# A graph-network layer on one core: two node streams laid in halves of the partitions, or in even and odd partitions

## The chip, the cores and the metric

The kernel runs on one core of a Trainium2 chip. The metric is the device time of one execution in microseconds; the time before is the median of three executions, 485.97 us (483.73 to 487.27).

## The reference

There are 12500 nodes with 128 features (`x`) and 412500 edges with 48 features (`edge_attr_48`), and each edge has a receiving node `dst`. The edges come sorted by `dst`.

```
agg = segment_sum(edge_attr_48, dst, 12500)          # 12500 x 48
h   = relu(layernorm(x))                             # 12500 x 128
u   = graph_globals[0]                               # one vector of 64 for all nodes
hid = relu(concat([h, agg, u]) @ W1 + b1)            # 12500 x 256
out = x + hid @ W2 + b2                              # 12500 x 128
```

Everything is float32.

## The kernel before

**Edges.** The edges are cut into 403 chunks of 1024, and these into two streams: stream 0 takes the first half of the chunks, stream 1 the second. A step (`contract`, L370) takes one chunk of each stream. A chunk's segment sum is a matmul of the edge features against a 0/1 matrix (`oh`, written by VectorE at L365 from the relative receiver numbers `rel`), gathered in PSUM (`ps`, L377); a step has 32 matmul instructions on TensorE. Six steps make a group; after a group VectorE adds `ps` into `aggT` (L393), which holds stream 0's sums in partitions 0 to 47 and stream 1's in partitions 64 to 111. There are 34 groups, so 204 steps. Edge features come in tiles `e` of two chunks, 384 KB each, through SyncE's DMA queue (L151); 15 tiles are in flight or in use at a time, and the next load is issued when TensorE has used a tile up.

**Nodes.** As the sums come in, the nodes are worked off in blocks. A block has 512 nodes (256 in the first and the last): half of them from the beginning of stream 0's nodes and half from stream 1's, which lie `END` rows farther in memory. There are 25 such blocks and one of 212 nodes from the middle. A node block is a tile of 128 partitions in which each partition holds four nodes in a row (2048 bytes); in the kernel before, partitions 0 to 63 hold stream 0's nodes and partitions 64 to 127 stream 1's. So one DMA of `x` (L221, on ScalarE's queue) or of results `ot` (L597, on SyncE's queue, the same that loads the edges) has two runs of 64 rows in device memory; the function `both` (L204) writes this access pattern with the two streams as its outermost dimension.

For a block, VectorE takes statistics (L517), ScalarE normalizes (`xn`, L513), TensorE transposes (`pt`, L529), ScalarE copies the transposed block from PSUM to `hT` (L533) with the nodes in order of partition and place in the partition, so that stream 0's nodes are the first half of the columns. TensorE makes the hidden layer in PSUM (`ph`): `hidden_x` (L553) from `hT`, `hidden_sums` (L566) from `aggT`, one half of the columns from each stream. ScalarE applies the bias and relu and writes `hid` (L573) with the columns sorted by place and then by partition. `output` (L585) uses `hid` as weights, 64 columns at a time, and `store` (L590) adds `x + b2` and issues the DMA of the results. `ot` has two buffers.

**Order.** The order on each engine is written out by hand: the loop at L717 goes through the steps; after each step a credit allows some of the node pieces (`pieces`, L613 on). The first three loads of `x` are issued on ScalarE's queue ahead of the first copies of `rel` (L438), which the first 0/1 matrices need.

Of the kernel before, what the change touches and what calls it, by code (L numbers as in the profile page):

```python
# [16 lines left out]
P = 128  # L17
# [4 lines left out]
def kernel(  # L22
# [31 lines left out]
    nc = tc.nc  # L54
    N, D = x.shape
# [33 lines left out]
    PH = P // 2  # L89
# [8 lines left out]
    NB2 = len(sizes)  # L98
    MID = sum(sizes) * PH
    NM = N - 2 * MID  # L100
    END = MID + NM
# [101 lines left out]

    def both(ap, a, r):  # L204

        return bass.AP(tensor=ap.tensor, offset=ap.offset + a * D, ap=[[END * D, 2], [r * D, PH], [1, r * D]])

    xs, xts, xns, xbs, hTs, hids, pos = {}, {}, {}, {}, {}, {}, {}
    x_loads = []

    def load_x(k):

        if k >= len(pairs):
            return
        xt = xp.tile([P, 2, R * D], F32, name="xt")
        xts[k] = xt

        def load(i, j):
            a, m, r = blocks[j]
            if j < NB2:  # L220
                nc.scalar.dma_start(xt[:, i, :r * D], both(x, a, r))  # L221
                return
            f = m - m % 16
            nc.scalar.dma_start(xt[:f, i, :r * D], rows_of(x, a, f, r))
            if f < m:
                nc.scalar.dma_start(xt[f:m, i, :r * D], rows_of(x, a + f * r, m - f, r))

        for i, j in enumerate(pairs[k]):
            xs[j] = xt[:, i].rearrange("p (r d) -> p r d", d=D)
            x_loads.append((k, lambda i=i, j=j: load(i, j), max(step, min(16 * k - 32, 114 + 4 * k))))  # L230
# [51 lines left out]
    with nc.allow_non_contiguous_dma(reason="a few hundred numbers, once"):  # L282
        for s in range(2):
            mid0 = C0[s] * CE
            n = min(NI, (E - mid0) // GE)
# [3 lines left out]
            for i in range(n, NI):  # L289
                m = mid0 + i * GE + GE // 2  # L290
# [233 lines left out]
    def transpose(j):  # L524
        _, m, nr = blocks[j]
        pt = pst.tile([P, R, P], F32, name="pt")
        xn = xns.pop(j)
        for r in range(nr):
            nc.tensor.transpose(pt[:, r, :m], xn[:m, r], ident[:m, :m])  # L529

        hT = mp.tile([P, BN], F32, name="hT", bufs=4)
        hTs[j] = hT[:, :m * nr]
        nc.scalar.copy(hTs[j].rearrange("d (p r) -> d p r", r=nr), pt[:, :nr, :m].rearrange("d r p -> d p r"))  # L533

    phs = {}

# [19 lines left out]
    def hidden_sums(j, q):  # L556

        at, m, nr = blocks[j]
        n = nr * PH
        if j < NB2:  # L560
            for s in range(2):
                a = s ^ q
                h = slice(s * HI, s * HI + DE)
                f = s * END + at + shift[s]
                for c in (0, HI):
                    nc.tensor.matmul(phs[j, a][c:c + HI, s * n:(s + 1) * n], w1a[h, a * P + c:a * P + c + HI],  # L566
                                     aggT[h, f:f + n], start=False, stop=True, skip_group_check=True)
        else:
            for c in (0, HI):
                nc.tensor.matmul(phs[j, q][c:c + HI, :NM], w1a[:K2, q * P + c:q * P + c + HI], mid[:K2],  # L570
                                 start=False, stop=True, skip_group_check=True)
        for a, h, f in ((q, 0, PH), (1 - q, PH, P)) if j < NB2 else ((q, 0, m),):
            nc.scalar.activation(hids[j][:, a, :nr, h:f],  # L573
                                 phs[j, a][:, h * nr:f * nr].rearrange("h (p r) -> h r p", r=nr),
                                 AF.Relu, bias=bias[:, a:a + 1])

    def output(j, r):
# [12 lines left out]
    def store(j):  # L590
        a0, m, nr = blocks[j]
        ot = mp.tile([P, R, D], F32, name="ot")
        nc.vector.tensor_tensor(ot[:m, :nr], pos.pop(j)[:m, :nr], xbs.pop(j)[:m, :nr], OP.add)  # L593
        k = m - m % 16
        od = ot[:, :nr].rearrange("p r d -> p (r d)")
        if j < NB2:
            nc.sync.dma_start(both(out, a0, nr), od)  # L597
            return
        nc.sync.dma_start(rows_of(out, a0, k, nr), od[:k])
        if k < m:  # L600
            nc.scalar.dma_start(rows_of(out, a0 + k * nr, m - k, nr), od[k:m])
# [20 lines left out]
    for j in range(NB2 + 1):  # L622
        if j == NB2:
            pieces.append((at[j], 0.0, lambda: copy_middle(0)))
        pieces.append((at[j], 0.6 * size[j], lambda j=j: hidden_sums(j, 0)))
        for q in [j + 2] if j + 3 < NB2 else [NB2 - 1, NB2] if j + 3 == NB2 else []:
            pieces.append((at[j], 0.8 * size[q], lambda q=q: turn(q)))
        pieces.append((at[j], 0.6 * size[j], lambda j=j: hidden_sums(j, 1)))
        if j < NB2:
            piece_x(j + 1, 0)  # L630
        for r in range(blocks[j][2]):
            pieces.append((at[j], 0.45, lambda j=j, r=r: output(j, r)))
        if j < NB2:
            piece_x(j + 1, 1)
# [22 lines left out]
    def turn(j):  # L657
        nonlocal turned
        while not normalized(j):
            next_part(True)  # L660
        transpose(j)
        turned = j
# [54 lines left out]
    for step in range(CG * NI + 3):  # L717
        i, k = divmod(step, CG)
# [30 lines left out]
    with tc.If(isbad >= 1):  # L749
# [63 lines left out]
        for k, js in enumerate(pairs):  # L813
            load_x(k)
            while x_loads:
                next_x()
            normalization(k)
            while parts:
                parts.pop(0)[2]()
            for j in js:  # L820
                transpose(j)
            for j in js:
                for a in range(NH):
                    hidden_x(j, a)
                for q in range(2):
                    hidden_sums(j, q)
                for r in range(blocks[j][2]):
                    output(j, r)
                store_late()
# [28 lines left out]
```

## Time and profile before

| what | before |
|---|---|
| median of three executions | 485.97 us |
| the profiled execution's own time | 485.91 us |
| its span | 484.1 us |
| granted TensorE clock, mean | 0.868 |
| TensorE matmul, VectorE, ScalarE busy | 341.8, 242.6, 123.6 us |
| DMA bytes, mean rate | 95.39 MB, 197 GB/s |

The span is the time between the first and the last instruction; the execution's own time is 1.8 us longer. The busy time of an engine is the union of its instructions. The DMA share is the mean over the core's 16 DMA engines: a share of 0.13 is what two engines of sixteen give when they are always busy (2/16 = 0.125).

### The profile page before, as it was taken

The page shows a single profiled execution, that of the slowest core. Times are in us where ns is not written, and L with a number is a line of the kernel's source. Part 1 is how long each engine was busy: PE and PEld are TensorE (multiplying, and loading weights), DVE is VectorE, ACT ScalarE, POOL GpSimd, SP SyncE. Part 2 cuts the span into 40 slices and gives each one's busy share as a digit, 9 for nine tenths or more (in the row PEclk, how much of TensorE's full clock was granted, in tenths as well). Part 3 has the DMA queues.
Part 4 walks back from the last instruction along what each step waited for, and adds up shares of the span by engine and source line. Part 5 has one row for each costly group of instructions (what it writes and reads, how often), then busy time and mean ns, then how long its engine had stood idle before and what let it go on. Part 6 is the DMA issues. An engine that isn't in the chain of part 4 may idle for free.

```text
span 484.1 us, 17713 instructions
## 1 busy us (share of the span) xinstructions
PE 341.8 (71%) x8037; PEld 272.4 (56%) x8038; DVE 242.6 (50%) x415; ACT 123.6 (26%) x296; POOL 15.5 (3%) x54
## 2 busy tenths in 40 slices
PE   6476839839796609949578706964956996599982
PEld 5475718727575408748456605744834864387751
DVE  1687516914763605825555524751734663767230
ACT  2143121423122105042023003321214131252220
POOL 9200000000000000000000000000000000000000
PEclk9986978978989958979969776995985999799997
DMA  8729594993566565765655765594665767786111
GB/s 240 252 80 268 175 290 123 318 301 122 184 207 199 198 183 190 244 229 172 210 177 175 234 201 196 179 313 140 197 206 171 237 204 221 218 253 237 56 40 43
DMA packets 62441, 95.39 MB, mean 197 GB/s; under 512 B 3755, under 2 KB 55831, under 8 KB 62356
## 3 DMA queue, kind: packets, MB, share of 16 engines
q1 hardware_dynamic: 58590, 87.16, 57.4%
q10 hardware_dynamic: 3382, 6.51, 3.6%
q8 instruction: 65, 1.06, 0.9%
q0 software_dynamic: 384, 0.49, 0.4%
q14 instruction: 20, 0.16, 0.1%
HBM read 87.74 MB, written 6.40 MB: 194 GB/s over the span
## 4 chain that ended last, share of the span: by engine, by line
DMA 56%; PE 32%; ACT 4%; DVE 3%; issue 1%; ACTq 1%; SPq 1%; POOL 0%; DVEq 0%; POOLq 0%
DMA e<-in_edge_attr_dram 45%; PE ps L377 17%; DMA xt<-in_x_dram 6%; PE po L585 6%; PE ph L553 5%; DMA out_dram<-ot 4%; PE ph L566 3%; DVE oh L365 2%; ACT xn L513 2%; ACT hid L573 1%; PE pt L529 1%; ACTq L221 1%; SPq L151 1%; DVE ot L593 0%; PE po L336 0%
## 5 line engine op out<-in xcount | busy, mean ns | idle before, releaser
L377 PEld LDWEIGHTS ps<-oh,e 128*48 128x48 f32 x6448 | 189.1, 133 | 85.7 <-issue 49.7
L377 PE MATMUL ps<-oh,e 128*48 128x44 f32 (+1 forms) x6448 | 198.8, 224 | 31.6 <-DMA e<-in_edge_attr_dram 20.0
L365 DVE TENSOR_TENSOR oh<-iota,rel 128x2816 f32<-128x2816 f32 (+3 forms) x72 | 149.8, 2100 | 26.6 <-ACT rel L439 25.6
L585 PE MATMUL po<-w,hid 128*64 128x128 f32 (+1 forms) x784 | 66.6, 295 | 26.2 <-ACT hid L573 26.0
L393 DVE TENSOR_TENSOR aggT<-aggT,ps 48x201 f32 (+1 forms) x68 | 24.4, 359 | 111.3 <-PE ps L377 79.9
L513 ACT ACTIVATE xn<-xt,sh,sc 128x128 f32<-128x128 f32 (+1 forms) x100 | 42.9, 485 | 112.9 <-DMA e<-in_edge_attr_dram 96.1
L585 PEld LDWEIGHTS po<-w,hid 128*64 128x64 f32 (+1 forms) x784 | 49.9, 148 | 29.0 <-ACT hid L573 27.9
L573 ACT ACTIVATE hid<-ph,bias 128x256 f32<-128x256 f32 (+2 forms) x102 | 41.5, 458 | 80.8 <-PE ph L566 65.9
L566 PE MATMUL ph<-aggT,w1a 48*64 48x256 f32 (+1 forms) x400 | 36.0, 421 | 34.3 <-ACT hid L573 28.4
L553 PE MATMUL ph<-hT,w1h 128*64 128x512 f32 (+2 forms) x208 | 58.5, 633 | 0.0
L593 DVE TENSOR_TENSOR ot<-po,xb 128x512 f32<-128x512 f32 (+2 forms) x26 | 17.4, 671 | 40.1 <-PE po L585 35.1
L529 PE MATMUL pt<-ident,xn 128*128 128x128 f32 (+1 forms) x100 | 19.6, 303 | 22.9 <-ACT xn L513 13.7
L517 DVE BATCH_NORM_STATS2 st<-xt 128x6 f32<-128x128 f32 (+1 forms) x100 | 23.6, 281 | 22.5 <-DMA xt<-in_x_dram 22.5
L566 PEld LDWEIGHTS ph<-aggT,w1a 48*64 48x64 f32 x400 | 11.6, 139 | 40.2 <-ACT hid L573 33.9
L503 ACT ACTIVATE sc<-va,eps 128x8 f32<-128x8 f32 (+3 forms) x15 | 4.5, 299 | 94.8 <-DVE va L502 94.8
L529 PEld LDWEIGHTS pt<-ident,xn 128*128 128x128 f32 (+1 forms) x100 | 11.3, 145 | 27.0 <-ACT xn L513 16.6
L533 ACT COPY hT<-pt 128x512 f32<-128x512 f32 (+2 forms) x26 | 14.4, 553 | 14.6 <-PE pt L529 8.1
L547 DVE TENSOR_TENSOR xb<-xt,b_sb 128x1024 f32<-128x1024 f32 (+3 forms) x15 | 15.6, 1038 | 0.1
L553 PEld LDWEIGHTS ph<-hT,w1h 128*64 128x64 f32 x208 | 13.5, 151 | 0.8 <-issue 0.6
L445 PE MATMUL pt<-ident,df 108*128 108x108 f32 (+3 forms) x36 | 6.6, 312 | 9.8 <-ACT hT L533 9.7
L445 PEld LDWEIGHTS pt<-ident,df 108*128 108x128 f32 (+3 forms) x36 | 4.9, 203 | 10.6 <-ACT hT L533 9.8
L438 ACT COPY rel<-pt 128x216 f32<-128x216 f32 (+3 forms) x9 | 4.0, 444 | 20.2 <-issue 10.9
(89 smaller groups left out, 89.8 us busy)
## 6 DMA issues: line engine op xcount, KB each, us to landing
e<-in_edge_attr_dram SPq DMA_DIRECT2D x200, 384.0 KB
xt<-in_x_dram ACTq DMA_DIRECT2D x23, 256.0 KB
out_dram<-ot SPq DMA_DIRECT2D x23, 256.0 KB
di<-in_dst_dram SPq DMA_DIRECT2D x4, 216.0 KB
e<-in_edge_attr_dram SPq DMA_DIRECT2D x2, 192.0 KB
di<-in_dst_dram SPq DMA_DIRECT2D x2, 180.0 KB
di<-in_dst_dram SPq DMA_DIRECT2D x2, 144.0 KB
xt<-in_x_dram ACTq DMA_DIRECT2D x2, 128.0 KB
```

The lines of the kernel that those rows point to most:

```text
L365: nc.vector.tensor_tensor(hots[i][:, at:at + n * Q * w].rearrange("p (h q w) -> p h q w", h=n, w=w)[:, :, q], iota[:, None, None, :w].to_b ...
L377: nc.tensor.matmul(ps[s * HI:s * HI + DE, o:o + WID[k]], edges[c][0][:, t * DE:(t + 1) * DE], hot(i, s, k, t), start=(k == 0 and t == 0), ...
L393: nc.vector.tensor_tensor(to, to, acc[i % len(acc)][h, :wg], OP.add)
L513: nc.scalar.activation(xns[j][:m, r], xs[j][:m, r], AF.Relu, bias=sh[:m, c:c + 1], scale=sc[:m, c:c + 1])
L517: parts.append((k, None, lambda i=i, j=j, r=r: nc.vector.bn_stats(st[:m, i * nr + r, :], xs[j][:m, r, :])))
L529: nc.tensor.transpose(pt[:, r, :m], xn[:m, r], ident[:m, :m])
L547: nc.vector.tensor_tensor(xb[:m, :n, :nr], xts[k].rearrange("p i (r d) -> p i r d", d=D)[:m, :n, :nr], b2_sb[:m, None, None, :].to_broadca ...
L553: nc.tensor.matmul(phs[j, a][c:c + HI, :nr * m], w1h[:, a * P + c:a * P + c + HI], hTs[j], start=True, stop=False, skip_group_check=True)
L566: nc.tensor.matmul(phs[j, a][c:c + HI, s * n:(s + 1) * n], w1a[h, a * P + c:a * P + c + HI], aggT[h, f:f + n], start=False, stop=True, ski ...
L573: nc.scalar.activation(hids[j][:, a, :nr, h:f], phs[j, a][:, h * nr:f * nr].rearrange("h (p r) -> h r p", r=nr), AF.Relu, bias=bias[:, a:a ...
L585: nc.tensor.matmul(pos[j][c:k, r], hids[j][:, a, r, c:k], w2[:, a], start=(a == 0), stop=(a == NH - 1), skip_group_check=True)
L593: nc.vector.tensor_tensor(ot[:m, :nr], pos.pop(j)[:m, :nr], xbs.pop(j)[:m, :nr], OP.add)
```

## The change

The streams' nodes of a block change places within the tile. Partition 2i now holds what partition i held (stream 0), and partition 2i + 1 what partition 64 + i held (stream 1). Three places follow: the pattern of the DMAs of `x` and of results has the 64 rows as its outermost dimension and the two streams inside it; the copy to `hT` puts the even partitions' nodes in the first half of the columns and the odd ones' in the second, so that the matmuls of the hidden layer stay as they were; and the activation that writes `hid` writes each half of the columns to every second column instead of to 64 neighbours. Each engine has as many instructions as before, in the same order, and each DMA as many bytes in rows of the same length.

```diff
     def both(ap, a, r):
 
-        return bass.AP(tensor=ap.tensor, offset=ap.offset + a * D, ap=[[END * D, 2], [r * D, PH], [1, r * D]])
+        return bass.AP(tensor=ap.tensor, offset=ap.offset + a * D, ap=[[r * D, PH], [END * D, 2], [1, r * D]])
...
         hTs[j] = hT[:, :m * nr]
-        nc.scalar.copy(hTs[j].rearrange("d (p r) -> d p r", r=nr), pt[:, :nr, :m].rearrange("d r p -> d p r"))
+        n = 2 if j < NB2 else 1
+        nc.scalar.copy(hTs[j].rearrange("d (s p r) -> d s p r", s=n, r=nr),
+                       pt[:, :nr, :m].rearrange("d r (p s) -> d s p r", s=n))
...
-        for a, h, f in ((q, 0, PH), (1 - q, PH, P)) if j < NB2 else ((q, 0, m),):
-            nc.scalar.activation(hids[j][:, a, :nr, h:f],
-                                 phs[j, a][:, h * nr:f * nr].rearrange("h (p r) -> h r p", r=nr),
+        for a, s in ((q, 0), (1 - q, 1)) if j < NB2 else ((q, 0),):
+            k = 2 if j < NB2 else 1
+            f = m // k * nr
+            nc.scalar.activation(hids[j][:, a, :nr, s:m:k],
+                                 phs[j, a][:, s * f:(s + 1) * f].rearrange("h (p r) -> h r p", r=nr),
                                  AF.Relu, bias=bias[:, a:a + 1])
```

## The prediction

> **What bounds the kernel now.** I read the page's time slices first, then the table of windows, then the chain of waits, then ScalarE's timeline at the start.
>
> ```profile
> PE   6476839839796609949578706964956996599982
> ...
> DMA  8729594993566565765655765594665767786111
> ...
> q1 hardware_dynamic: 58590, 87.16, 57.4%
> q10 hardware_dynamic: 3382, 6.51, 3.6%
> q8 instruction: 65, 1.06, 0.9%
> ...
> DMA 56%; PE 32%; ACT 4%; DVE 3%; issue 1%; ACTq 1%; SPq 1%; POOL 0%; DVEq 0%; POOLq 0%
> ```
>
> The chain that ended last is 56% DMA, yet the DMA engines are only 57.4 + 3.6 + 0.9 + 0.4 + 0.1 = 62.4% busy, and TensorE falls to 3 or 4 tenths again and again. A bound of DMA with more than a third of it idle means either latency or uneven load. The table of windows tells which (columns: stretch, length, busy time and instructions of PE, PEld, DVE, ACT, POOL, then granted clock, DMA share, GB/s):
>
> ```profile
> 328.00:332.00 4.00, 0.00 (x0) 0.00 (x0) 0.00 (x0) 0.00 (x0) 0.00 (x0) 0.59 0.13 49
> 452.00:460.00 8.00, 8.00 (x179) 5.50 (x175) 2.96 (x12) 2.28 (x6) 0.00 (x0) 1.00 0.15 56
> 54.00:66.00 12.00, 7.83 (x222) 6.41 (x222) 8.06 (x16) 0.30 (x1) 0.00 (x0) 0.99 0.97 318
> 312.00:322.00 10.00, 7.92 (x212) 6.10 (x210) 8.25 (x15) 3.12 (x8) 0.00 (x0) 1.00 1.02 349
> ```
>
> From 328 to 332 every compute engine stands still, waiting for edges, while DMA moves 49 GB/s at a share of 0.13: two engines of sixteen. From 452 to 460 the edges are in, only results are being stored, and again it is about two (0.15, instruction fetches included). Where edges flow alone (54 to 66) the share is 0.97 at 318 GB/s: an edge load uses all sixteen. So a DMA of `x` or of results runs on two engines, and an edge tile has a sixteenth of its bytes on each of those two; it has not landed before they have come to it.
>
> Are these two engines full? Page part 6 lists 23 loads of `x` of 256 KB and 2 of 128 KB, and the same number of stores: 12.6 MB, at 49 GB/s 257 us. The edges, 202 tiles of 384 KB, are 79 MB; two sixteenths are 9.9 MB, at 49 GB/s 202 us. Together 459 of 484.1 us. These two engines are the bound of the whole kernel; nearly every long wait for edges is a wait for them. (That the edges are spread evenly is inferred from the share of 0.97.)
>
> The Trainium skill, "DMA: Bandwidth & Descriptors", section "Why a DMA increments its semaphore by 16 and not by 1", gives the count for both versions, where the trace can show only the first: the largest number up to 16 that divides the outermost dimension on both sides, so 2 before (2 and 128) and 16 after (64 and 128). No run here shows the second yet; by the rule the forecast below holds, and without it the third rival stays open.
>
> **The change, part by part.**
>
> *The DMAs.* The trace has two rows for how wide a transfer is: a pattern with 2 as its outermost dimension runs on two engines, the edge loads' pattern, with 128 partitions outermost, on all sixteen. The new pattern has 64, which can be dealt out to sixteen; I take sixteen for the fifty transfers, with two as the other end (rival 3). The number, bytes, row length and issuing queue stay. A transfer of 256 KB, 5.3 us at 49 GB/s, then takes 0.75 to 0.82 us at 349 to 318 GB/s plus its latency. The load per engine becomes the mean, 62.4% of 484.1 = 302 us. Bounds by rate: 95.39 MB at 349 and 318 GB/s give 273 and 300 us.
>
> *The start.* ScalarE's timeline:
>
> ```profile
> 5.42 11.10 ACTq L221 DMA_DIRECT2D xt<-in_x_dram  x3
> 16.56 0.24 ACT L438 COPY rel<-pt 128x48 f32<-128x48 f32 x1 [10.90 <-issue]
> ```
>
> Issuing three loads holds ScalarE for 11.1 us, since the two engines' queues are full; an unhindered issue takes 0.51 us (the median of L221), so 1.5 us. `rel` comes 9.6 us earlier, and with it the 0/1 matrices and the first `ps` matmul, which stood at 18.23 us: about 9 us. What is late next is the edges: at the 268 GB/s of the first 20 us some 2.4 MB, six tiles, are there by then, enough.
>
> *The copy to `hT`* (26 of 553 ns) reads two interleaved halves; its reading was already strided, so I take it at nothing. *The activation to `hid`* (102 of 458 ns) writes every second column. The trace has no such write. Dense: the copy to `hT` of 212 columns at 0.34 us; far apart: `rel`, 216 columns at 516 ns. The difference, 0.8 ns a column, bounds it: 0 to 0.2 us each, 0 to 21 us on ScalarE, which is busy 124 us and hides it. Without cover, at the end of the kernel where some eight stand on the path, it is 0 to 1.7 us. I take 0, the stride of two being nearest to dense.
>
> *A wait that is added.* The first `output` matmuls of a block read 64 neighbouring columns of `hid`, written before by one activation, now by two. Queued behind them on TensorE are the following `ps` matmuls. Between the last activation and them stands `hidden_x` (0.88 us in the chain), longer than two activations (0.84 us): nothing in midstream, about 0.1 us for each of three blocks at the end. On SyncE's, ScalarE's and GpSimd's queues nothing changes place.
>
> **The sum.** With the two engines relieved, TensorE is next. Its pace without waits stands in the chain (start, length, what):
>
> ```profile
> 298.31 0.71 PE ps L377 x32
> 299.02 0.89 PE po L585 x16
> ...
> 304.56 0.59 PE ph L566 x8
> 305.15 0.85 PE ps L377 x32
> 306.00 0.59 PE pt L529 x4
> ...
> 308.89 0.88 PE ph L553 x4
> 309.76 0.71 PE ps L377 x32
> ```
>
> From 298.31 to 309.76 it makes eight steps with all node work of one block: 11.45/8 = 1.43 us a step, at full clock. 202 steps' worth of matmuls (6448/32): 289 us. The transposes of `dst` come on top (L445, 6.6 us) and the first dozen steps have no node work; I let these cancel. But in that stretch DMA was half idle. Coupling costs something: TensorE was busy 19.57 of 20 us with DMA share 0.33 (440 to 460), but 18.53 and 18.19 with 0.82 and 0.77:
>
> ```profile
> 80.00:100.00 20.00, 18.53 (x524) 15.20 (x518) 15.26 (x26) 5.91 (x12) 0.00 (x0) 1.00 0.82 266
> 420.00:440.00 20.00, 18.19 (x524) 15.80 (x520) 13.60 (x24) 8.45 (x19) 0.42 (x1) 0.98 0.77 242
> 440.00:460.00 20.00, 19.57 (x491) 14.69 (x488) 8.68 (x25) 6.37 (x16) 0.00 (x0) 1.00 0.33 119
> ```
>
> That is 6.6%, 19 us. The end, from the last `ps` (458.8) to 484.1, is 25.3 us; in the chain a store on two engines holds an `ot` buffer there for 7.80 us, while the matmuls of the last block end at 474.9 instead of 476.4, so only 1.5 us go: 24. Sum: 9 + 289 + 19 + 24 = 341 us of span, plus 1.8 us around it: **343 us**, against 485.91 us for the profiled execution (the median, 485.97, is the same). DMA by itself: 2 + 302 to the last bytes, of which the last blocks' stores lie behind, then the end: about 329. VectorE, 242.6 us busy, is 71% of the new span and not the bound.
>
> On the clock: it fell to 0.66 from 280 to 300 and 0.74 from 320 to 340, where TensorE had long waits, and was 1.00 from 440 to 460, where it worked nearly without a break. The Trainium skill, "TensorE: Matmul & The Clock Gate", section "Part 1: The HAM clock gate", agrees (half clock after an idle window of about 3.4 us) and speaks against a full clock here: waits of that length that remain would keep the gate closing. By it the sum is 343 us if they go, near the first rival's time if they stay.
>
> **Rivals.**
>
> 1. *The clock stays as it is.* For: waits for edges may go on in shorter pieces; mean 0.868 before. Against: the waits come from two engines that are no longer overloaded. 289/0.868 = 333; 9 + 333 + 19 + 24 + 2 = 387 us.
> 2. *DMA remains the bound, by its busiest engine.* Instruction fetches (q8: 0.9% of sixteen engines, 70 us) come one at a time; if one engine carries them all, it has 302 - 4 + 70 = 368 us, and with the end 2 + 368 + 24 + 2 = 396 us. For: one engine is enough to hold a tile back. Against: nothing shows that one engine carries them.
> 3. *It doesn't do what it says*: the queue still cuts the transfer into two runs of engines. Then 459 us on the same two engines and 486 us. Against: the 128-partition edge loads are spread.
> 4. *Slower.* TensorE, now busy nearly all the time, is held at a low clock by its own load. 289/c + 54 passes 486 where c falls below 0.67; at half clock through 632 us. Place: the step loop from 20 us on. Against: clock 0.98 and 1.00 in the two rows from 420 to 460, with TensorE busy 37.8 of 40 us. From 0.67 downward it decides.
>
> **How the numbers follow.** Chances: forecast 0.78; the clock 0.09; the busiest engine 0.09; no effect 0.02; low clock 0.02. The range takes in the forecast without coupling (324), a start and DMA slightly better (318), and reaches past the first two rivals: 318 to 400. A measurement of this kernel tells about 1% from no change. Faster by over 1%: 0.78 + 0.09 + 0.09 = 0.96; within: 0.02; slower: 0.02.
>
> **What would show it.** Right: the DMA share no longer stays at 0.13 with compute engines idle; three loads of `x` issued within 2 us and the first `ps` matmul near 9 us; the chain mostly TensorE; mean clock above 0.93; rate near 280 GB/s; `hid` near 458 ns. Wrong: stretches of DMA share 0.13 remaining (rival 3); a share near 0.06 with TensorE waiting (one engine, rival 2); clock below 0.9 with TensorE busy (1 or 4); `hid` at 0.6 us or more (the write's price).

## The result and the profile after

The changed kernel takes 354.14 us (350.9 to 356.11, four executions) against 485.45 us before (483.73 to 487.27): a ratio of 0.7288, 95% interval 0.7227 to 0.7349. In a second measurement it was 0.7240 (0.7204 to 0.7276). Forecast were 343 us, in a range of 318 to 400. The profiled execution took 354.23 us, its span 352.4 us; 131.7 us of span are gone. Executions of one kernel differ by up to 3%: a ratio is taken from the fast ones alone (within 1.5% of the fastest), a time in us is the median of all.

The lines of the page that answer to those shown of before (TensorE and DMA in 40 slices, the DMA queues, the chain that ended last):

```profile
PE   7794979999999899899998889989999999999881
...
DMA  7999997999999998998799899999989898921010
...
q1 hardware_dynamic: 58940, 87.16, 75.9%
q10 hardware_dynamic: 3732, 6.51, 5.6%
q8 instruction: 65, 1.06, 1.3%
...
PE 74%; DVE 11%; issue 6%; ACT 4%; DMA 2%; SPq 1%; DVEq 0%; ACTq 0%
```

The bytes are the same. TensorE falls to 4 tenths once, in the fourth slice (26 to 35 us), and stays at 7 or more after that until the last slice; DMA is at 7 to 9 tenths until the edges are in; and the chain has turned round: DMA from 56% to 2%, TensorE from 32% to 74%. The DMA engines' mean load, 83.4% of 352.4 us (75.9 + 5.6 + 1.3 + 0.5 + 0.1), is 294 us; before it was 302. So there is no less DMA work; it is spread.

The windows (stretch, length, busy time and instructions of PE, PEld, DVE, ACT, POOL, granted clock, DMA share, GB/s):

```profile
20.00:40.00 20.00, 14.98 (x382) 12.27 (x378) 17.46 (x51) 9.38 (x24) 0.00 (x0) 0.91 1.06 374
240.00:260.00 20.00, 19.93 (x532) 16.17 (x529) 14.91 (x24) 7.42 (x20) 0.00 (x0) 1.00 0.91 292
320.00:340.00 20.00, 17.93 (x353) 12.43 (x347) 6.47 (x18) 4.81 (x13) 0.00 (x0) 1.00 0.10 34
```

From 240 to 260 us TensorE is busy 19.93 of 20 us at full clock with DMA at a share of 0.91; that is the best of these rows, the worst from 60 to 300 us has 17.57 busy. The only long stretch with little DMA is the end, where the edges are in; no DMA stands on the chain there any more.

ScalarE at the start, and TensorE's first and last `ps` matmuls in the timeline (start, length):

```profile
6.74 2.98 ACTq L221 DMA_DIRECT2D xt<-in_x_dram  x3
9.76 0.24 ACT L438 COPY rel<-pt 128x48 f32<-128x48 f32 x1 [4.09 <-DMA e<-in_edge_attr_dram]
...
11.44 4.06 PE L377 MATMUL ps<-oh,e 128*48 128x44 f32 x96 [3.14 <-DVE oh L365]
...
327.93 0.91 PE L377 MATMUL ps<-oh,e 128*48 128x37 f32 x16
```

Three loads of `x` are issued in 2.98 us instead of 11.10. The first `ps` matmul is at 11.44 us (18.23 before), the last ends at 328.8 (458.8), and 23.6 us follow.

ScalarE's groups by shape (count, busy us, mean ns), then the issue of `x` (minimum, median, maximum in ns):

```profile
L577 ACT ACTIVATE hid<-ph,bias 128x256 f32<-128x256 f32 x92 | 39.9, 489 | 68.6 <-PE ph L568 68.6
L534 ACT COPY hT<-pt 128x512 f32<-128x512 f32 x23 | 13.3, 580 | 8.5 <-PE pt L529 8.5
...
L221 ACTq DMA_DIRECT2D xt<-in_x_dram x25: 542/542/750, 6.7 to 277.3; - x25
```

The strided write of `hid` costs 22 ns an instruction (467 before), the copy to `hT` 2 ns (578 before), and no issue of `x` takes longer than 0.75 us, where before the longest took 7.6.

### The profile page after: what moved, and what is told of

Its sections match the earlier page's. It is cut to its first block, busy times and chain, and to the rows that moved or that the text cites. A ratio compares the mean times of both kernels' runs of the same rounds, so it can differ in the third digit from the quotient of the medians.

```text
span 352.4 us, 17715 instructions
## 1 busy us (share of the span) xinstructions
PE 317.1 (90%) x8037; PEld 254.5 (72%) x8038; DVE 242.0 (69%) x415; ACT 124.8 (35%) x296; POOL 15.5 (4%) x54
## 3 DMA queue, kind: packets, MB, share of 16 engines
q1 hardware_dynamic: 58940, 87.16, 75.9%
## 4 chain that ended last, share of the span: by engine, by line
PE 74%; DVE 11%; issue 6%; ACT 4%; DMA 2%; SPq 1%; DVEq 0%; ACTq 0%
PE ps L377 37%; PE po L589 13%; PE ph L555 11%; PE ph L568 8%; DVE oh L365 6%; PE pt L529 4%; ACT hid L577 2%; DMA e<-in_edge_attr_dram 2%; DVE st L517 1%; ACT xn L513 1%; DVE aggT L393 1%; PE pt L445 1%; DVE ot L597 1%; ACT sc L503 0%; DVE va L502 0%
## 5 line engine op out<-in xcount | busy, mean ns | idle before, releaser
L377 PEld LDWEIGHTS ps<-oh,e 128*48 128x48 f32 x6448 | 177.9, 127 | 64.0 <-issue 55.0
L377 PE MATMUL ps<-oh,e 128*48 128x44 f32 (+1 forms) x6448 | 188.9, 218 | 14.7 <-issue 10.9
L577 ACT ACTIVATE hid<-ph,bias 128x256 f32<-128x256 f32 (+2 forms) x102 | 43.3, 479 | 75.5 <-PE ph L568 73.7
L589 PE MATMUL po<-w,hid 128*64 128x128 f32 (+1 forms) x784 | 58.5, 278 | 1.2 <-ACT hid L577 1.1
L555 PE MATMUL ph<-hT,w1h 128*64 128x512 f32 (+2 forms) x208 | 53.7, 591 | 0.0
L589 PEld LDWEIGHTS po<-w,hid 128*64 128x64 f32 (+1 forms) x784 | 43.4, 137 | 3.7 <-ACT hid L577 2.6
L568 PE MATMUL ph<-aggT,w1a 48*64 48x256 f32 (+1 forms) x400 | 34.1, 398 | 2.9 <-ACT hid L577 2.8
L529 PE MATMUL pt<-ident,xn 128*128 128x128 f32 (+1 forms) x100 | 17.9, 296 | 7.0 <-ACT xn L513 6.9
L534 ACT COPY hT<-pt 128x512 f32<-128x512 f32 (+2 forms) x26 | 14.4, 554 | 9.5 <-PE pt L529 9.5
L568 PEld LDWEIGHTS ph<-aggT,w1a 48*64 48x64 f32 x400 | 10.9, 132 | 8.5 <-ACT hid L577 3.6
L555 PEld LDWEIGHTS ph<-hT,w1h 128*64 128x64 f32 x208 | 11.8, 142 | 1.1 <-issue 0.9
L336 PE MATMUL po<-ident 128*128 128x128 f32 x24 | 5.2, 387 | 2.0 <-POOL ident masks.py:199 2.0
```

Of the source, the lines that this page charges most:

```text
L377: nc.tensor.matmul(ps[s * HI:s * HI + DE, o:o + WID[k]], edges[c][0][:, t * DE:(t + 1) * DE], hot(i, s, k, t), start=(k == 0 and t == 0), ...
L555: nc.tensor.matmul(phs[j, a][c:c + HI, :nr * m], w1h[:, a * P + c:a * P + c + HI], hTs[j], start=True, stop=False, skip_group_check=True)
L577: nc.scalar.activation(hids[j][:, a, :nr, s:m:k], phs[j, a][:, s * f:(s + 1) * f].rearrange("h (p r) -> h r p", r=nr), AF.Relu, bias=bias[ ...
L589: nc.tensor.matmul(pos[j][c:k, r], hids[j][:, a, r, c:k], w2[:, a], start=(a == 0), stop=(a == NH - 1), skip_group_check=True)
```

## The experiments

All ratios are to the kernel before, measured beside it. "In halves" means that each DMA is issued as two, one for each half of the partitions.

| kernel | us | ratio (95%) |
|---|---|---|
| changed kernel, second measurement | 354.77 | 0.7240 (0.7204 to 0.7276) |
| both transfers in two halves | 371.56 | 0.7624 (0.7576 to 0.7673) |
| only results in halves (x on two engines) | 425.74 | 0.8775 (0.8740 to 0.8810) |
| only x in halves (results on two engines) | 388.03 | 0.7991 (0.7961 to 0.8020) |
| halves, but every fourth block on two engines | 387.89 | 0.7971 (0.7927 to 0.8015) |
| x twice | 371.83 | 0.7606 (0.7567 to 0.7645) |
| x twice but in the first blocks | 366.73 | 0.7539 (0.7517 to 0.7561) |
| half of the last matmul | 342.56 | 0.7032 (0.6989 to 0.7076) |
| first x issued later | 354.51 | 0.7307 (0.7277 to 0.7337) |
| two combs (two DMAs, each to every second partition) | 364.17 | 0.7450 (0.7419 to 0.7482) |
| two halves, first x issued later | 370.62 | 0.7626 (0.7606 to 0.7645) |
| only results in halves, x ahead | 436.52 | 0.9009 (0.8987 to 0.9031) |

### Is it the number of engines, or the new order of the rows?

In the layout of before, each transfer is issued as two, so that 64 becomes the outermost dimension without any change of places.

```diff
-                nc.scalar.dma_start(xt[:, i, :r * D], both(x, a, r))
+                for s in range(2):
+                    nc.scalar.dma_start(xt[s * PH:(s + 1) * PH, i, :r * D], stream(x, a, r, s))
...
-            nc.sync.dma_start(both(out, a0, nr), od)
+            for s in range(2):
+                nc.sync.dma_start(stream(out, a0, nr, s), od[s * PH:(s + 1) * PH])
```

`stream(ap, a, r, s)` is the 64 rows of one stream.

> The layout of before is kept (streams in the halves of the partitions, hid written densely), but each DMA of x and of results is issued as two, one for each stream, of 64 rows. Theory (number of engines): each half goes over sixteen engines, so the load per engine is that of the changed kernel: 350 to 362 us; the 50 further issues of about 0.54 us on ScalarE's and SyncE's queues are hidden. Rival (it is the pairing of near and far rows, or the dense reading of neighbouring partitions, that helps): close to the time before, 470 to 487 us.

371.56 us. The rival is out: with the old layout and a dense `hid`, 114 of the 131 us are gained by the pattern of the DMAs alone, although their number doubles. But the time lies 10 us above the theory's range; the next sections follow that up.

### One of the two alone

The same edit for the results only, and for `x` only.

> The layout of before; only the DMAs of results are issued as two of 64 rows, x stays as before. Theory (load of two engines): 9.9 MB of edges and 6.3 MB of x at 49 GB/s are 330 us on the two engines, plus the end of 24 us, with some coupling: 355 to 395 us. Rival (what costs is that ScalarE is held while it issues x): nearly the time before, 450 us or more.

> The layout of before; only the DMAs of x are issued as two of 64 rows, results stay as before. Theory (load of two engines): the same 330 us on the two engines, so about the same time as with only the results divided, 355 to 395 us, the start 7 us earlier and the end some 2 us longer. Rival (ScalarE held by issuing x): nearly all of the gain, 350 to 360 us.

425.74 and 388.03 us. With only `x` divided the time is in the range; with only the results divided it is 31 us above it. Neither rival fits: ScalarE's holding would have given about 355 us with `x` divided. Against the run with both divided, results on two engines cost 16 us, `x` on two engines 54 us, both together 114 us (485.88 - 371.56), more than the sum of 71. That fits two engines that are full only with both (an estimated 459 us of load with both, 330 with one). That equal bytes cost so unequally, the load alone doesn't explain. What held SyncE's issues of edges (line, releaser, us in total, times, longest) in the run with `x` on two engines, and then in the one with results on two:

```profile
SPq L151 <- DMA xt<-in_x_dram: 98.3, 19, 8.6
```

```profile
SPq L151 <- DMA out_dram<-ot: 38.5, 14, 3.6
```

The same work waits 98.3 us for `x` in the one and 38.5 for results in the other. The two runs also differ in when these transfers are made. Step 50 begins at 119.3 us with `x` on two engines, at 99.2 with results on two and at 98.8 with both divided: 20 of the 54 us are lost by then, after ten loads of `x` issued 1 to 33 us apart, and nothing in the other run, where the first of four stores comes at 52 us. Whether this bunching makes the difference was not tried.

### Is x late?

In the run with `x` on two engines VectorE's statistics waited 18.2 us for `x`. So there the loads of `x` were made due ten steps earlier, and the normalization was to stay at its old step.

```diff
-            ... max(step, min(16 * k - 32, 114 + 4 * k))))
+            ... max(step, min(16 * k - 42, 104 + 4 * k))))
...
-                begun in came and ... and came[begun] <= step - 8)):
+                begun in came and ... and came[begun] <= step - 18)):
```

> The run with only the results divided (x on two engines, 425.7 us), with each load of x due ten steps earlier and the normalization at the same step as there. Theory (x on two engines costs more than results on two because its transfer, some 14.5 us in the chain, is longer than its lead, and normalization and TensorE wait for it): 390 to 410 us. Rival (x costs more because it is on another queue and halves the two engines' pace for the edges): 420 to 430 us.

436.52 us: slower, and outside both ranges. The waits of VectorE's statistics for `x` are gone from the list of waits, and SyncE's issues wait as they did, now 109.6 us for `x`:

```profile
SPq L151 <- DMA xt<-in_x_dram: 109.6, 16, 8.7
...
SPq L602 <- DMA xt<-in_x_dram: 20.8, 5, 6.7
```

The loss lies at the start. The first five loads of `x` are issued at the same steps in both runs, so for them the edit only held the normalization back. ScalarE's normalization in the run with `x` on two engines, and then in this one (instructions, duration, first and last start):

```profile
L517 ACT ACTIVATE xn<-xt,sh,sc x100: 477/484/500, 30.0 to 388.2; 128x128 f32<-128x128 f32 x96, 53x128 f32<-53x128 f32 x4
```

```profile
L517 ACT ACTIVATE xn<-xt,sh,sc x100: 477/485/497, 40.4 to 399.0; 128x128 f32<-128x128 f32 x96, 53x128 f32<-53x128 f32 x4
```

It begins 10.4 us later and ends 10.8 us later. Step 20 begins at 68.0 us instead of 56.6, and from there to the end both runs take the same time, 365.9 and 366.7 us, although most loads in between are issued 7 to 16 steps earlier. So it is not lateness of `x`: earlier loads gain nothing. The rival, competition between the two queues on the two engines, fits that, but wasn't tried by itself (by giving `x` the edges' queue). Why `x` costs more than three times what results cost on two engines is left open.

### Does a transfer on two engines cost in proportion, or only above a limit?

Both transfers in halves, except in every fourth block (6 of 25).

```diff
+                if j % 4 == 1:
+                    nc.scalar.dma_start(xt[:, i, :r * D], both(x, a, r))
+                    return
```

and the same for the results.

> The layout of before; x and results are issued as two of 64 rows except in every fourth block (6 of 25), where they stay on two engines. Theory (load of two engines, no cost below the pace of TensorE): 9.9 + 3.1 MB at 49 GB/s are 266 us, below TensorE's 320 us, so 350 to 364 us. Rival (each transfer on two engines costs its own delay, in proportion): 354 plus a quarter of the 131 us, about 385 us.

387.89 us. Against its proper base, the run with two halves (371.56), 16 us for 24% of the transfers, where proportion would be 27 us of 114. The theory that nothing is lost while the two engines' total load stays below TensorE's time is refuted: with a load of 266 us in 384 there were still waits (the chain by line):

```profile
PE ps L385 34%; PE po L593 12%; PE ph L561 10%; DMA xt<-in_x_dram 10%; PE ph L574 7%; DMA e<-in_edge_attr_dram 7%; PE pt L537 3%; DVE oh L373 1%; ACT hid L581 1%; ACT xn L521 1%; PE pt L453 1%; DVE st L525 1%; ACTq L229 0%; DVE ot L601 0%; ACT hT L541 0%
```

In the run with two halves, with no transfer on two engines, the same line reads:

```profile
PE ps L382 32%; PE po L590 11%; PE ph L558 10%; DMA e<-in_edge_attr_dram 8%; PE ph L571 7%; DVE oh L370 3%; PE pt L534 3%; ACT xn L518 2%; ACT hid L578 2%; DMA xt<-in_x_dram 2%; DVE st L522 1%; DMA di<-in_dst_dram 1%; DVE ot L598 1%; PE pt L450 1%; ACTq L226 1%
```

So the edges' share has not risen; that of `x` has, from 2% to 10%. Its pieces on the chain (start, length) all lie in the first 65 us; the first and the third are the first two loads left on two engines:

```profile
8.60 18.32 DMA xt<-in_x_dram
32.11 5.84 DMA xt<-in_x_dram
50.62 13.92 DMA xt<-in_x_dram
```

Step 30 begins at 78.6 us here and at 69.0 in the run with two halves (spans 383.9 and 372.0), so most of the loss between these two profiles is there early; what each later transfer cost can't be told from them. A mean load is a lower bound here, no forecast.

### What bounds the changed kernel: TensorE or DMA?

DMA work was added: each load of `x` a second time, into a tile that nobody reads. And TensorE work was taken away: half of the last matmul.

```diff
                 nc.scalar.dma_start(xt[:, i, :r * D], both(x, a, r))
+                again = xp.tile([P, R * D], F32, name="again", bufs=2)
+                nc.scalar.dma_start(again[:, :r * D], both(x, a, r))
```

```diff
-        for a in range(NH):
+        for a in range(1):
...
-                nc.tensor.matmul(pos[j][c:k, r], hids[j][:, a, r, c:k], w2[:, a], start=(a == 0), stop=(a == NH - 1),
+                nc.tensor.matmul(pos[j][c:k, r], hids[j][:, a, r, c:k], w2[:, a], start=(a == 0), stop=True,
```

> The changed kernel with each DMA of x issued a second time into a tile that nobody reads: 6.3 MB more. Theory (TensorE sets the pace, DMA has room): 0 to 5 us more than the changed kernel. Rival (DMA still sets the pace): 6.6% more bytes, 15 to 20 us more.

> The changed kernel without the second half of the hidden columns in the last matmul: 392 of its 784 matmul instructions are left out, so the results lack that half. They cost 1.81 us per 32 in the chain, so 22 us. Theory (TensorE sets the pace): 15 to 22 us less than the changed kernel. Rival (DMA or VectorE sets the pace): 0 to 5 us less.

> The changed kernel once more, as the measure for the other runs of this call: 351 to 356 us.

371.83, 342.56 and 354.77 us. The added transfers cost 5.1% (0.7606/0.7240; 4.4% against the first measurement's 0.7288), as the rival said; the removed matmuls gave 10 (by the ratios) to 12 of 22 us, between both ranges. But doubling also put three more issues ahead of `rel`, so it was repeated without the first three blocks:

> The changed kernel with the DMAs of x issued a second time into a tile that nobody reads, but not in the first three blocks, so that nothing more stands ahead of rel: 5.6 MB more. Theory (most of the 17 us that the doubling cost came from the issues ahead of rel, and TensorE sets the pace afterwards): 353 to 361 us. Rival (the bytes cost it, DMA sets the pace as well): 366 to 372 us.

366.73 us, 4.1% more (0.7539/0.7240; 3.4% against 0.7288) for 5.9% more bytes: most of the cost is not the start's. Bytes and issues are not parted by this. The 22 added issues hold ScalarE for 16.1 us, and the run with two combs below, with 50 issues more and no more bytes, is 8 to 10 us above the changed kernel. The stretch from 60 to 300 us of the changed kernel, of x twice, and of half of the last matmul:

```profile
60.00:300.00 240.00, 227.99 (x6115) 183.45 (x6113) 178.96 (x287) 90.32 (x212) 0.18 (x1) 1.00 0.92 300
```

```profile
60.00:300.00 240.00, 222.09 (x5883) 178.09 (x5880) 173.94 (x271) 85.86 (x203) 0.18 (x1) 0.99 0.95 312
```

```profile
60.00:300.00 240.00, 219.75 (x5902) 172.81 (x5896) 184.82 (x288) 93.77 (x219) 0.18 (x1) 0.97 0.93 307
```

With more DMA work TensorE is busy 6 us less in these 240, and with less of its own 8 us less; DMA rises to 0.95 and 0.93. Part of the 6 us is spread: in the second measurement's profile of the changed kernel itself TensorE is busy 224.51 us, with DMA at 0.91. The changed kernel stands near two limits, TensorE at 95% and DMA at 92%, and neither alone sets the pace: work on DMA's side costs time, and work taken from TensorE gives back only half of its own. What TensorE waits for in midstream the profile doesn't show (10.9 us before `ps`, with no releaser).

### The start

In the changed kernel the three issues of `x` still stand ahead of `rel`. They were put behind it, in the changed kernel and in the one with two halves.

```diff
-    for _ in range(3):
-        next_x()
     stir(5)
     spread(0, dfs[0], start=True)
+    for _ in range(3):
+        next_x()
```

> The changed kernel with the first three loads of x issued on ScalarE's queue after the first copies of rel instead of before. In the changed kernel these issues hold rel until 9.76 us although the transposes are done at about 7.4. Theory (the start is on the path): first ps matmul 2 to 3 us earlier, 1 to 3 us less time. Rival (the start is hidden by the edges' arrival, or x comes late for the first block): no difference, or 1 to 2 us more.

> The run with two halves again, with the first loads of x issued after the first copies of rel. With two halves the six issues ahead of rel put the first ps matmul at 16.5 us, against 11.4 in the changed kernel. Theory (the start makes 5 of the 17 us between the two): 364 to 368 us. Rival (the start is absorbed within the first 20 steps): 370 to 374 us.

354.51 and 370.62 us: no difference in either, as the rivals said. The first `ps` matmul does come earlier (9.3 instead of 11.4 us; 9.2 instead of 16.5), but by step 20 the changed kernel is at 44.8 us and the one with the later issue at 44.3; the two runs with halves are level by step 50 (98.8 and 100.2 us). What sets the pace of the first steps was not isolated; DMA moves 374 GB/s there, its highest rate.

### Why two halves cost 17 us more than the change

Two DMAs for every one, and each to one half of the partitions. To part these, the changed kernel's layout was used with two DMAs, each to every second partition.

```diff
+                for s in range(2):
+                    nc.scalar.dma_start(xt[s::2, i, :r * D], stream(x, a, r, s))
...
+            for s in range(2):
+                nc.sync.dma_start(stream(out, a0, nr, s), od[s::2])
```

> The layout of the changed kernel, with each DMA of x and of results issued as two, one for each stream, of 64 rows to every second partition. As many DMAs as in the run with two halves (371.6 us), as many engines, but each reaches over all partitions instead of one half of them. Theory (transfers to one half of the partitions are slow: their packets took 119 and 105 ns there, 92 and 87 in the changed kernel): packets of 95 ns or less, and 355 to 364 us. Rival (the number of DMAs and issues costs it): packets and time as with two halves, 368 to 374 us.

364.17 us, at the edge of the theory's range and halfway between the two. The packets (means of those of 1024 and 2048 bytes) took 101 ns for `x` and 84 ns for results, so only the results' are below 95. The DMA queues of the two halves (with the later start, span 369.3 us):

```profile
q1 hardware_dynamic: 59340, 87.16, 76.1%
q10 hardware_dynamic: 4132, 6.51, 7.0%
```

and of the combs (span 367.7 us; this execution took 369.53 us, the median is 364.17):

```profile
q1 hardware_dynamic: 59340, 87.16, 72.5%
q10 hardware_dynamic: 4132, 6.51, 5.8%
```

Per engine the halves take 83.1% of 369.3 = 307 us, the combs 78.3% of 367.7 = 288 us, the changed kernel 81.5% of 352.4 = 287 us. These are all bytes of the two queues, the edges among them. So with transfers to and from one half of the partitions the DMA engines need 19 us more for the same bytes, and with every second partition they don't: 14.4 us more on SyncE's queue (q1) and 4.5 on ScalarE's (q10). Not all of it falls on the divided transfers: the edges' own packets of 1536 bytes, which the edit doesn't touch, took 78.1 ns in the mean beside the halves and 74.9 beside the combs, 10 us on each engine. The halves against the combs are worth 0.0176 in the ratio (0.7626 - 0.7450), 8.5 us; the rest, 0.745 against 0.724 to 0.729 (8 to 10 us), comes with twice the number of DMAs: SyncE spends 32.9 us issuing results instead of 16.1, ScalarE 30.2 issuing `x` instead of 14.7. Which of these two holds the path was not tried. In the combs' profile the first `ps` matmul is at 17.7 us, as six issues stand ahead of `rel`, and step 20 begins at 52.1 us against 44.8 in the changed kernel: about half of the difference between these two profiles (15 us) is there by then.

## Why the prediction was right or wrong

- **The bound: right.** Two overloaded engines, not DMA as a whole; both divided into 64 rows gives 0.762 with nothing else changed but the number of DMAs, and 16 engines' mean load was as forecast (302 predicted, 294 measured). The load is no forecast by itself, though: with 330 us of it on the two engines the runs took 388 and 426 us. The row from 54 to 66 us is not edges alone, as packets of `x` move from 63 on; up to 63 the share is 0.94 at 305 GB/s, so its reading stands.
- **The width of the new pattern: right.** No row of 20 us up to 300 us has a DMA share below 0.84, and a load of `x` is issued in 0.54 us instead of up to 7.6. Three stores of 256 KB near the end move their packets in 0.83 to 1.55 us, for which the forecast had 0.75 to 0.82 and latency; before, two in a row took 10.6 us. Of the packets of `x` at most 6 are in flight at once before and 17 after. The rule of the Trainium skill ("DMA: Bandwidth & Descriptors", section "Why a DMA increments its semaphore by 16 and not by 1"), which gave 16 for 64 and 128, agrees with the runs: all forms with 64 outermost for `x` and results came to 0.72 to 0.76. The trace doesn't number the engines, so it shows many more than two, not the count of 16.
- **The start: a term too good, and worth nothing.** Forecast 9 us for the first `ps` matmul, measured 11.44, since the issues began at 6.74 us, not 5.42, and took 2.98 us instead of 1.5. "Six tiles are there by then, enough" didn't hold as a ground for counting the gain: the later-start runs show that a still earlier first matmul is absorbed, by step 20 in the changed kernel and by step 50 with two halves.
- **The pace: too fast.** 289 + 19 = 308 us forecast from the first to the last `ps`, 317.4 measured (328.8 - 11.44). From step 30 on it was 1.545 us a step (264.2 us for 171), against 1.525 with the coupling term, so that term was nearly right. The first 30 steps took 52.3 us, 1.74 each, 6.5 us more than forecast. The forecast had no term for them, as it let the transposes of `dst` and the missing node work cancel; the runs show waits there, 6.9 us for `xn` and 3.5 for `oh` up to 60 us, and a clock of 0.74, 0.91 and 0.83 in the three rows of 20 us. What would shorten them was not tried, except the start, which didn't.
- **The end: right.** 24 forecast, 23.6 measured.
- **The strided write and the added wait: right.** 22 ns an activation, within 0 to 0.2 us, 2 us of ScalarE in all and hidden; TensorE waited 1.1 us for `hid` before the output matmuls in all.
- **The sum.** 341 forecast for the span, 352.4 measured: 2.4 from the start, 9 from the pace, less 0.4 at the end.
- **The rivals.** The clock didn't stay: mean 0.964, and 1.00 in every row of 20 us from 60 to 340 us, where TensorE is idle for 2.4 us of 20 at most. A single busiest engine would have given 396 us and left TensorE waiting at a low DMA share; no such stretch is there. No effect and slower are out by the time itself. That VectorE is not the bound fits its 11% of the chain, but no run changed its work. What the forecast understated is that DMA is not merely next but nearly level: 5.9% more bytes, with their issues, cost 3.4 to 4.1%.

## What to carry to other kernels

When the chain says DMA and the DMA engines are a third idle, look for stretches in which a small share stays constant while everything waits: a share of 0.13 was two engines of sixteen, and the pattern's outermost dimension of 2 had put them there. Laying out a tile so that the outermost dimension of both sides of one DMA is large gave more than cutting the DMA in two, here because packets were dearer with the two halves and the number of DMAs doubled. And a transfer confined to few engines can cost even when their total load would fit into the span: 6 of 25 blocks cost 16 us.

## What was not expected of the hardware

- With `x` and results moved to or from one half of the partitions at a time, all bytes of the two queues occupied each DMA engine 307 us; with every second partition, 288 us. About half of the difference stands in the edges' packets, whose own pattern was the same.
- On two engines, `x` (ScalarE's queue) cost 54 us and results of the same size (SyncE's, the edges' queue) 16 us; issuing `x` earlier gained nothing after step 20. Unexplained.
- From 20 to 40 us the sixteen engines moved 374 GB/s, more than the rows of the kernel before from which the forecast took its bounds (318 and 349 GB/s).
